# Retention's rotated queries and keys from one projection and a partition shuffle, and a plan that knows of wide GpSimd operations

## The chip, the cores and the metric

The kernel runs on one core of a Trainium2 chip. A core has a matrix engine (TensorE, PE in the profile), three engines for elementwise work (VectorE: DVE, ScalarE: ACT, GpSimd: POOL) and SyncE (SP), which here issues DMAs. The engines run side by side, each through its own instructions strictly in order, and wait for each other by semaphores. All work is in fp32. The metric is the device time of one execution in microseconds; the time before is 453.98 us, the median of three runs (452.66 to 454.3).

## The reference

Eight sequences of 256 tokens, 128 features each, go through eight residual steps, each behind a layer norm:

```
x = x + causal_attention(layernorm(x))     # 64-dimensional keys, one head
x = x + ffn_relu(layernorm(x))             # 512 hidden; ends in a layer norm of its own
x = x + linear_attention(layernorm(x))
x = x + ffn_relu(layernorm(x))
x = x + retention(layernorm(x))            # 16 heads
x = x + ffn_silu(layernorm(x))             # 384 hidden, int8-like weights
x = x + softmax_attention(layernorm(x))    # 16 heads of 8, LoRA weights
x = x + ffn_silu(layernorm(x))
```

The change is in retention. There queries and keys are rotated with the position:

```
def _rotate_every_two(x):
    x1 = x[..., ::2]
    x2 = x[..., 1::2]
    return jnp.stack((-x2, x1), axis=-1).reshape(x.shape)

def _theta_shift(x, sin, cos):
    return x * cos + _rotate_every_two(x) * sin

q = x @ q_w + q_b
k = (x @ k_w + k_b) * SCALING
qr = _theta_shift(q, sin, cos)
kr = _theta_shift(k, sin, cos)
```

So each rotated value needs its own value and that of its neighbour in the pair. The decay over positions is folded into the tables of sines and cosines, and the sign of the rotation into the table of sines.

## The kernel before

**Tiling.** The tokens are cut into four groups (GROUPS) of 512 tokens, two sequences each. A group's x is one tile of 128 partitions (tokens) by 4 x 128. Layers work on its transpose, 128 features by 512 tokens. Results of TensorE come in eight PSUM banks of 512 columns (`bank`), and are moved to SBUF by ScalarE or VectorE (L414 in `copied`). Other buffers come from stores: `work` (28), `small` (16), `wide` (6), `probs` (6), and the spread tiles `r_spread` and `l_spread`, which DMAs fill so that each head's queries and keys stand on partitions of their own (L761).

**The plan.** The order of all instructions is worked out when the program is built. Each layer of each group is a generator (`layers(g)`) that yields steps: an engine, or a choice of engines (`either`), and a cost in microseconds. The class `Plan` runs these generators against a clock of its own. At each turn it takes the step that can start first, and among those that can start on the same engine the one with the lowest rank; ranks are the hand-set numbers in RANKS, one for each group and layer, with FIRST, LAST and LATE for the rest. A step taken is written out at once, so that each engine's instruction order is the order in which the plan took the steps. For `either` the engine that could start first gets the work. Weights are prepared by threads with start times of their own (the `plan.start` lines at the end of `hybrid`). The plan's costs only set the order: on the chip every instruction waits for its data and nothing else.

**What lies near the change**, by line:

- `layernorm` (L503): statistics on VectorE (L511, L512), then four small operations on GpSimd (L518, L519, L522, L523; with `quick` the first two on VectorE), then per tile of 128 columns the normalisation, on ScalarE (L529) or VectorE (L534). `transposed` (L542) turns the result by TensorE (L550).
- Wide operations of GpSimd (128x512, or 128x272 in L903): `add_row_to` (L581), the biases and gamma of `ffn_relu` (L716, L752), the running sums of retention's states (L903), and some sums in `rotated` (L802).
- `ffn_relu`: up (L723, evicted by L726 or L728), down (L736, L742), a layer norm, gamma, and the residual sum L754 on VectorE.
- `retention` (L778): `rotated(i)` for queries (i = 0) and keys (i = 1). The weights hold four projections: queries, queries with the columns of each pair swapped, and the same for keys. Each is one matmul of 512 columns (L792), and VectorE adds the bias and multiplies by the table of cosines or sines while it moves the result out of PSUM (L794). GpSimd or VectorE adds the two parts (L802). Then come values (L822, L827), gates (L810, L812), the transposed keys (L875), states (L894, L881), scores by heads (L859, masked by L844), sums within and over chunks (L917, L939, L947) and a normalisation over the head (`finished`: L965 to L977, a square root by Newton steps, L767 to L776, transposition L986, gate L993, output L1002).
- Softmax attention: scores (L1135), maxima (L1156), exponentials (L1190), weighted sums (L1207), turned by L1220; projections L1249; FFN with silu: L1049, L1055, L1065.

Of the kernel before, what the change touches and what calls it, by code (L numbers as in the profile page):

```python
# [52 lines left out]
    "linear": [(32, 2, P), (P, D)],  # L53
    "retention_qk": [(P, 4, P), (P, 4, S), (P, 4)],
    "retention_vo": [(P, 512), (P, 256), (P, 2), (P, HEADS, VONE), (P, 2, D), (P, D)],
# [9 lines left out]
NEW_MODE = 0.09  # L65
LOAD = 0.1
ARRIVALS = (3.1, 5.1, 6.8, 8.3)
LEEWAY = 0.03


RANKS = [
    [-4.13, -2.77, -1.79, -1.45, 1.42, 1.01, -0.24, 3.83],
    [-1.82, 0.93, 5.08, 2.15, 1.79, 4.87, 0.66, 0.66],
    [-0.37, 1.61, -4.13, 2.32, 5.49, -4.05, 3.4, 4.38],
    [3.42, 6.69, 6.1, 9.09, 1.61, 0.82, 1.3, 1.92],
]
FIRST, LAST = -4.34, 9.59
LATE = 1.56


def of_act(n):
    return 0.05 + n / 1160
# [49 lines left out]
class Plan:  # L132
# [4 lines left out]
    def __init__(self):  # L137
        self.free = {e: 0.0 for e in (PE, ACT, DVE, POOL, SP)}
        self.steps = {e: [] for e in self.free}
        self.stores, self.untils, self.sleeping = [], [], []  # L140
        self.table = None
        self.mode = None
        self.current = None
        self.count = 0
        self.now = 0.0
# [20 lines left out]
    def put(self, store, *items, later=0.0):  # L166
        for item in items:
            self.count += 1
            store.items.append((self.current.after() + later, self.count, item))
# [30 lines left out]
    def joined(self, th):  # L200
        if th.join and all(j.done for j in th.join):
# [3 lines left out]
            self.go.append(th)  # L205

    def run(self):
        self.go = []
        while True:
# [12 lines left out]
            for e, queue in self.steps.items():  # L222
                if queue:
                    start = max(self.free[e], min(q[0] for q in queue))
                    if best is None or start < best[0]:
                        best = (start, e, None)
# [14 lines left out]
            if s is not None:  # L241
# [7 lines left out]
                continue  # L249
            able = [q for q in self.steps[e] if q[0] <= start]  # L250

# [16 lines left out]
            th.t, th.last = start + us, e  # L268
            self.free[e] = th.t
            self.resume(th, e)  # L270
        stuck = [s.waiting for s in self.stores if s.waiting] + self.untils
# [3 lines left out]
def step(engine, us, table=None, mode=None):  # L275
    return ("step", ((engine, us, table),), mode)


def either(*choices):
    return ("step", tuple((e, us, None) for e, us in choices), None)  # L280


def get(store, n=1):
    return ("get", store, n)


def join(threads):
    return ("join", list(threads))
# [11 lines left out]
def hybrid(ctx: ExitStack, tc: tile.TileContext, t: dict, out: bass.AP):  # L300
# [104 lines left out]
    def tokens(row, n):  # L405

        return row.unsqueeze(1).to_broadcast([P, n, row.shape[1]])
# [95 lines left out]
    def layernorm(src, y, quick=False):  # L503
# [21 lines left out]
        def half(tiles):  # L525
            for i in tiles:
                e = yield either((ACT, 0.39), (DVE, 0.25))
                if e == ACT:
                    nc.scalar.activation(  # L529
                        y[:, i, :], src[:, i, :], AF.Identity, bias=shift[:, i : i + 1],  # L530
                        scale=rstd[:, i : i + 1],
                    )
                else:
                    nc.vector.tensor_scalar(  # L534
                        y[:, i, :], src[:, i, :], mv[:, i, 0:1], rstd[:, i : i + 1],
                        ALU.subtract, ALU.mult,
                    )
# [41 lines left out]
    def add_row_to(g, row):  # L579
        yield step(POOL, 1.23)  # L580
        nc.gpsimd.tensor_tensor(x[g], x[g], tokens(row, NT), ALU.add)  # L581
# [126 lines left out]
    def ffn_relu(g):  # L708
# [5 lines left out]
        def biases():  # L714
            yield step(POOL, 1.23)
            nc.gpsimd.tensor_tensor(y4, y4, tokens(b2, NT), ALU.add)  # L716
            yield from add_row_to(g, beta)
# [32 lines left out]
        yield from layernorm(y4, y4)  # L750
        yield step(POOL, 1.23)
        nc.gpsimd.tensor_tensor(y4, y4, tokens(gamma, NT), ALU.mult)  # L752
        yield step(DVE, 0.6)
        nc.vector.tensor_tensor(flat(x[g]), flat(x[g]), y[:, :N], ALU.add)  # L754
# [23 lines left out]
    def retention(g):  # L778
# [4 lines left out]
        def rotated(i):  # L783

            part2 = yield get(work)
            a = qk[:, i, :], part2[:, :N]
            ps = yield get(bank, 2)

            def part(k):
                n = 2 * i + k  # L790
                yield step(PE, 0.86)
                nc.tensor.matmul(ps[k], w_ret_qk[:, n, :], yT[:, :N], start=True, stop=True)  # L792
                yield step(DVE, 0.66)
                nc.vector.scalar_tensor_tensor(  # L794
                    a[k].rearrange("p (b s) -> p b s", b=2), ps[k].rearrange("p (b s) -> p b s", b=2),
                    b_ret_qk[:, n : n + 1], tokens(rot_tab[:, n, :], 2), ALU.add, ALU.mult,
                )
                put(bank, ps[k])

            yield join([spawn(part(k)) for k in range(2)])  # L800
            e = yield either((POOL, 1.25), (DVE, 0.63))
            (nc.gpsimd if e == POOL else nc.vector).tensor_tensor(a[0], a[0], a[1], ALU.add)  # L802
            put(work, part2)
# [64 lines left out]
        def states(b, v, state):  # L868
# [32 lines left out]
            for n in range(1, 3):  # L901
                yield step(POOL, 0.73)
                nc.gpsimd.tensor_tensor(  # L903
                    state[n][:, :HV], state[n][:, :HV], state[n - 1][:, :HV], ALU.add
                )
# [51 lines left out]
        def finished(b, o, sq):  # L957
# [5 lines left out]
            den, var, root, tmp = (st[:, 32 * n : 32 * n + 32] for n in range(4))  # L963
            yield step(DVE, 1.03)
            nc.vector.tensor_scalar(  # L965
# [4 lines left out]
            put(work, sq)  # L970
            yield step(DVE, 2.35)
            newton_root(root, var, tmp)
            y = yield get(work)
            yield step(DVE, 0.6)
            nc.vector.scalar_tensor_tensor(
# [356 lines left out]
    for g in range(GROUPS):  # L1332
        plan.start(layers(g), g, ARRIVALS[g])
    plan.start(constants(), LAST, 31.1)
    plan.start(linear_weights(), LAST, 11.9)
    plan.start(retention_weights(), LAST, 47.5)
    plan.start(silu_weights(), LAST, 22.5)
    plan.start(softmax_weights(), LAST, 19)
    plan.start(pairs_of_scores(), FIRST, 0.0)
# [31 lines left out]
def _layout(i):  # L1371
    def swapped(a):

        return a.reshape(*a.shape[:-1], -1, 2)[..., ::-1].reshape(a.shape)

    q, qb, k, kb = (i[f"L1_attn_a_{n}"] for n in ("q_w", "q_b", "k_w", "k_b"))
    order = _by_head_rows()
    q, qs, k, ks = (a[..., order] for a in (q, swapped(q), k, swapped(k)))
    qb, qbs, kb, kbs = (a[order] for a in (qb, swapped(qb), kb, swapped(kb)))
    lora = {"q": order, "k": order, "v": np.arange(D)}  # L1380
# [5 lines left out]
    def chunks(a):  # L1386
# [15 lines left out]
        "retention_qk": (  # L1402
            np.stack([q, qs, k, ks], 1), _retention_tables(), np.stack([qb, qbs, kb, kbs], 1),
        ),
# [45 lines left out]
```

## Time and profile before

| | us |
|---|---|
| median of three runs | 453.98 |
| the profiled execution | 452.34 |
| its span | 450.5 |
| 16 projections for retention, L792, 32 instructions | 16.1 busy on TensorE |
| 16 rotations, L794 | 12.0 busy on VectorE |
| 8 sums, L802 | 6.8 busy on GpSimd (5), 3.0 on VectorE (3) |
| normalisations, L534 on VectorE (71) and L529 on ScalarE (89) | 30.6 and 38.9 busy |
| wide operations of GpSimd: L581 (16), L716 (8), L752 (8), L903 (16) | 20.4, 10.2, 10.2 and 12.3 busy |

A matmul in fp32 shows as two or more instructions, which overlap; the time of one is best read from when it and the next start. The groups of the profile give for each line the engine, the operation, the tiles (out<-in), the shapes, the count, the busy time, the mean of one, and the idle time of the engine just ahead of them with what ended it. The first and the last part of a page name the chain of work that ended last: followed back from the end, at each step, to whatever released it.

In the 40 slices of the span TensorE is at 9 tenths or more in all but the first and a few in the first 40%, GpSimd is busiest in the first third:

```
PE   7899899899999998999999999999999999999996
DVE  6997989787869985789998498869678656738443
ACT  3669735553433623513574773467963854783561
POOL 4154558765523562042222020320111100101101
```

### The profile page before, as it was taken

The numbers are of one execution on the slowest core, as the hardware profiler recorded it, in microseconds if no ns is written. First come the engines' busy times: TensorE is split into PE (matmuls) and PEld (weight loads), VectorE is DVE, ScalarE is ACT, GpSimd is POOL, SyncE is SP. The second block draws the span as 40 slices with busy tenths as digits, with TensorE's granted clock in tenths as the row PEclk, the third lists the DMA queues.
The fourth block names the chain that finished last, engine by engine and source line by source line (L and its number), as shares of the span: only waits on it lengthen the run. The fifth ranks groups of instructions, "written<-read, shape, count | busy, mean of one in ns | idle before, by whom it ended". The sixth has DMA issues, their size and how long they took to land.

```text
span 450.5 us, 13165 instructions
## 1 busy us (share of the span) xinstructions
PE 427.5 (95%) x5360; PEld 300.0 (67%) x5360; DVE 345.9 (77%) x992; ACT 245.0 (54%) x492; POOL 133.5 (30%) x239
## 2 busy tenths in 40 slices
PE   7899899899999998999999999999999999999996
PEld 6777677657677575685755665776765866566666
DVE  6997989787869985789998498869678656738443
ACT  3669735553433623513574773467963854783561
POOL 4154558765523562042222020320111100101101
PEclk9999899999999998999999999999999999999999
DMA  7300000003000300350000520000110001010001
GB/s 275 132 1 1 1 1 0 1 1 48 4 2 17 34 4 3 49 49 2 5 3 4 61 37 3 4 4 4 25 26 14 13 27 26 9 20 1 15 1 35
DMA packets 8043, 10.90 MB, mean 24 GB/s; under 512 B 1000, under 2 KB 6888, under 8 KB 7984
## 3 DMA queue, kind: packets, MB, share of 16 engines
q1 hardware_dynamic: 7904, 9.94, 10.7%
q8 instruction: 42, 0.69, 0.6%
q14 instruction: 17, 0.14, 0.1%
q10 hardware_dynamic: 80, 0.13, 0.1%
HBM read 4.56 MB, written 1.05 MB: 12 GB/s over the span
## 4 chain that ended last, share of the span: by engine, by line
PE 72%; DVE 18%; issue 4%; POOL 2%; ACT 2%; DMA 1%; SPq 0%; POOLq 0%; DVEq 0%; ACTq 0%
PE bank L1135 16%; PE bank L1207 7%; PE bank L1065 5%; PE bank L1049 5%; PE bank L859 4%; PE bank L736 4%; PE bank L1055 4%; PE bank L723 3%; DVE work L534 3%; DVE small L511 3%; PE bank L917 3%; DVE small L512 2%; PE bank L894 2%; PE bank L591 2%; PE bank L1220 2%
## 5 line engine op out<-in xcount | busy, mean ns | idle before, releaser
L1156 DVE TENSOR_REDUCE small<-bank 128x2 f32<-128x512 f32 x128 | 80.7, 684 | 15.2 <-PE bank L1135 14.4
L1135 PE MATMUL bank<-l_spread 32*128 32x256 f32 x1024 | 86.5, 401 | 0.0
L518 POOL TENSOR_SCALAR small<-small 128x4 f32<-128x4 f32 (+1 forms) x40 | 11.8, 295 | 242.7 <-DVE small L512 227.2
L1190 ACT ACTIVATE probs<-bank 128x512 f32<-128x512 f32 x128 | 67.7, 601 | 28.9 <-PE bank L1135 28.7
L414 ACT COPY work<-bank 128x512 f32<-128x512 f32 (+3 forms) x77 | 37.1, 492 | 68.1 <-PE bank L550 27.2
L1135 PEld LDWEIGHTS bank<-l_spread 32*128 32x128 f32 x1024 | 54.5, 184 | 25.7 <-issue 11.3
L522 POOL TENSOR_TENSOR small<-small,mhalf 128x4 f32<-128x4 f32 (+1 forms) x45 | 43.4, 965 | 6.8 <-DVE small L519 6.8
L529 ACT ACTIVATE work<-x,small 128x128 f32<-128x128 f32 x70 | 30.6, 487 | 26.6 <-POOL small L523 26.5
L511 DVE BATCH_NORM_STATS2 small<-x 128x6 f32<-128x128 f32 x128 | 34.7, 271 | 3.9 <-DMA x<-in_x 3.5
L414 DVE COPY work<-bank 128x256 f32<-128x256 f32 (+3 forms) x35 | 17.9, 521 | 22.8 <-PE bank L1207 12.3
L1207 PE MATMUL bank<-probs,l_values 128*32 128x256 f32 x512 | 33.2, 384 | 1.1 <-DVE work L1057 0.6
L736 PE MATMUL bank<-c_relu,work 128*128 128x128 f32 x256 | 32.4, 278 | 1.2 <-DVE work L728 1.2
L736 PEld LDWEIGHTS bank<-c_relu,work 128*128 128x128 f32 x256 | 30.3, 192 | 4.7 <-issue 2.4
L512 DVE BATCH_NORM_AGGREGATE small<-small 128x2 f32<-128x6 f32 x160 | 29.1, 182 | 5.5
L723 PE MATMUL bank<-work,c_relu 128*128 128x512 f32 x64 | 32.2, 618 | 0.1
L726 ACT ACTIVATE work<-bank,c_relu 128x512 f32<-128x512 f32 x26 | 17.9, 687 | 16.7 <-PE bank L723 15.7
L586 DVE TENSOR_TENSOR x<-bank,x 128x256 f32<-128x256 f32 (+1 forms) x36 | 16.1, 450 | 13.0 <-PE bank L1065 7.1
L1049 PE MATMUL bank<-work,c_ints 128*128 128x256 f32 (+1 forms) x72 | 25.3, 463 | 0.7 <-ACT work L414 0.7
L1065 PE MATMUL bank<-c_ints,work 128*128 128x128 f32 x192 | 24.6, 279 | 0.5 <-ACT work L414 0.5
L1051 ACT ACTIVATE work<-bank 128x256 f32<-128x256 f32 (+1 forms) x36 | 15.7, 454 | 16.7 <-PE bank L1049 16.4
L1065 PEld LDWEIGHTS bank<-c_ints,work 128*128 128x128 f32 x192 | 22.9, 192 | 2.7 <-issue 1.1
L1055 PE MATMUL bank<-work,c_ints 128*128 128x256 f32 (+1 forms) x72 | 24.6, 458 | 0.0
(151 smaller groups left out, 797.6 us busy)
## 6 DMA issues: line engine op xcount, KB each, us to landing
r_spread<-wide SPq DMA_DIRECT2D x32, 64.0 KB
l_spread<-wide SPq DMA_DIRECT2D x32, 64.0 KB
out<-x SPq DMA_DIRECT2D x8, 128.0 KB
c_retention_qk<-in_retention_qk SPq DMA_DIRECT2D x1, 770.0 KB
x<-in_x SPq DMA_DIRECT2D x3, 256.0 KB
c_retention_vo<-in_retention_vo SPq DMA_DIRECT2D x1, 713.0 KB
c_relu<-in_relu SPq DMA_DIRECT2D x1, 706.0 KB
c_ints<-in_ints SPq DMA_DIRECT2D x1, 576.0 KB
```

What stands on the lines that cost most here:

```text
L414: (nc.scalar.copy if e == ACT else nc.vector.tensor_copy)(dst, src)
L511: nc.vector.bn_stats(stats[:, i, :], src[:, i, :])
L522: nc.gpsimd.tensor_tensor(rstd, rstd, minus_half[:, :nt], ALU.pow)
L723: nc.tensor.matmul(ps, w1[:, c * P : (c + 1) * P], yT[:, :N], start=True, stop=True)
L736: nc.tensor.matmul(ps[:, n * D : (n + 1) * D], h[c][:, i * P : (i + 1) * P], w2[:, c, :], start=(c == 0), stop=(c == 3),)
L1049: nc.tensor.matmul(ps[:, :n], w_gate[:, cols], yT[:, :n], start=True, stop=True)
L1055: nc.tensor.matmul(ps[:, :n], w_up[:, cols], yT[:, :n], start=True, stop=True)
L1065: nc.tensor.matmul(ps[:, (i - first) * D : (i - first + 1) * D], h[c][:, i * P : (i + 1) * P], w_down[:, c, :], start=(c == 0), stop=(c == 2),
L1135: nc.tensor.matmul(to[k][:, n * S : (n + 1) * S], seq.spread[rows, j, of_keys, n * P : (n + 1) * P], seq.spread[rows, j, 1 - of_keys, :], ...
L1156: nc.vector.tensor_reduce(nmax[:, h2 % 4 // 2, 2 * (h2 % 2) + k, :], ps[k].rearrange("p (m s) -> p m s", m=2), AX.X, ALU.max, negate=True,)
L1190: nc.scalar.activation(p[:, k, :], ps[k], AF.Exp)
L1207: nc.tensor.matmul(o[32 * i : 32 * (i + 1), (j % 2) * S : (j % 2 + 1) * S], seq.v[:, c, VONE * h : VONE * h + 32], seq.p[h2][0][:, k, c * ...
```

## The change

The change has three parts.

1. In `rotated` queries and keys are projected once each, with their biases added on the way out of PSUM by ScalarE or VectorE. The swapped values are then made in SBUF by a shuffle of partitions on VectorE: features are laid out so that the two of a pair stand four partitions apart within 32. Two multiplications by the tables and the sum follow, each on GpSimd or VectorE. One PSUM bank is held instead of two. The packed weights, the biases and the layout lose their swapped halves, so that this load has 641 KB instead of 770.

2. The plan has a mark `PORT`. Wide operations of GpSimd carry it, and so do the steps of VectorE that read and write SBUF alone: L534, L754, L965 to L977 with the Newton steps, the shuffle, and the multiplications and sums of `rotated`. While a marked step runs on GpSimd in the plan's time, a marked step on VectorE can't start there; `either` then may give it to the other engine, or another step is taken first.

3. The numbers that steer the plan are others: all RANKS, FIRST, LAST, LATE, LEEWAY (how much later than its last reader a score bank counts as free) and the start times of the threads for weights and constants.

```diff
@@ class Plan
+        self.port = 0.0
...
+    def ready(self, engine, q):
+        return max(q[0], self.port) if engine == DVE and q[1].mode == PORT else q[0]
...
-                    start = max(self.free[e], min(q[0] for q in queue))
+                    start = max(self.free[e], min(self.ready(e, q) for q in queue))
...
-            able = [q for q in self.steps[e] if q[0] <= start]
+            able = [q for q in self.steps[e] if self.ready(e, q) <= start]
...
             self.free[e] = th.t
+            if e == POOL and th.mode == PORT:
+                self.port = th.t
...
@@ layernorm
-                e = yield either((ACT, 0.39), (DVE, 0.25))
+                e = yield either((ACT, 0.39), (DVE, 0.25), mode=PORT)
...
@@ add_row_to; the same mark at L715, L751, L753, L902, L964, L971, L974
-        yield step(POOL, 1.23)
+        yield step(POOL, 1.23, mode=PORT)
...
@@ retention, rotated(i)
-            part2 = yield get(work)
-            a = qk[:, i, :], part2[:, :N]
-            ps = yield get(bank, 2)
-
-            def part(k):
-                n = 2 * i + k
-                yield step(PE, 0.86)
-                nc.tensor.matmul(ps[k], w_ret_qk[:, n, :], yT[:, :N], start=True, stop=True)
-                yield step(DVE, 0.66)
-                nc.vector.scalar_tensor_tensor(
-                    a[k].rearrange("p (b s) -> p b s", b=2), ps[k].rearrange("p (b s) -> p b s", b=2),
-                    b_ret_qk[:, n : n + 1], tokens(rot_tab[:, n, :], 2), ALU.add, ALU.mult,
+            part1, part2 = qk[:, i, :], (yield get(work))
+            ps = yield get(bank)
+            yield step(PE, 0.86)
+            nc.tensor.matmul(ps, w_ret_qk[:, i, :], yT[:, :N], start=True, stop=True)
+            e = yield either((ACT, of_act(N)), (DVE, of_dve(N)))
+            if e == ACT:
+                nc.scalar.activation(part1, ps, AF.Identity, bias=b_ret_qk[:, i : i + 1])
+            else:
+                nc.vector.tensor_scalar(part1, ps, b_ret_qk[:, i : i + 1], None, ALU.add)
+            put(bank, ps)
+
+            yield step(DVE, 0.65, mode=PORT)
+            nc.vector.stream_shuffle(part2[:, :N], part1, [p ^ KDIM // 2 for p in range(32)])
+
+            def times(k, a):
+                e = yield either((POOL, 1.25), (DVE, 0.63), mode=PORT)
+                a = a.rearrange("p (b s) -> p b s", b=2)
+                (nc.gpsimd if e == POOL else nc.vector).tensor_tensor(
+                    a, a, tokens(rot_tab[:, 2 * i + k, :], 2), ALU.mult
                 )
-                put(bank, ps[k])
-
-            yield join([spawn(part(k)) for k in range(2)])
-            e = yield either((POOL, 1.25), (DVE, 0.63))
-            (nc.gpsimd if e == POOL else nc.vector).tensor_tensor(a[0], a[0], a[1], ALU.add)
+
+            yield join([spawn(times(k, a)) for k, a in enumerate((part1, part2[:, :N]))])
+            e = yield either((POOL, 1.25), (DVE, 0.63), mode=PORT)
+            (nc.gpsimd if e == POOL else nc.vector).tensor_tensor(
+                part1, part1, part2[:, :N], ALU.add
+            )
             put(work, part2)
...
@@ the numbers of the plan
-LEEWAY = 0.03
+LEEWAY = 0.04
...
-    [-4.13, -2.77, -1.79, -1.45, 1.42, 1.01, -0.24, 3.83],
+    [-0.77, -1.96, -6.09, -0.44, -1.22, -2.97, -2.46, 4.75],
...
-FIRST, LAST = -4.34, 9.59
-LATE = 1.56
+FIRST, LAST = -3.5, 11.25
+LATE = 0.91
...
-    plan.start(retention_weights(), LAST, 47.5)
-    plan.start(silu_weights(), LAST, 22.5)
-    plan.start(softmax_weights(), LAST, 19)
+    plan.start(retention_weights(), LAST, 15.6)
+    plan.start(silu_weights(), LAST, 16.5)
+    plan.start(softmax_weights(), LAST, 43.2)
```

In the built program the instructions of retention's rotation fall like this; apart from them, 21 normalisations stand on ScalarE that stood on VectorE, and the order on every engine is another from the first layers on.

| | before | after |
|---|---|---|
| projections on TensorE | 16 | 8 |
| evictions with the bias | 16 on VectorE, times the table | 7 on ScalarE, 1 on VectorE |
| shuffles on VectorE | 0 | 8 |
| multiplications by a table | in the eviction | 9 on GpSimd, 7 on VectorE |
| sums | 5 on GpSimd, 3 on VectorE | 4 on GpSimd, 4 on VectorE |
| normalisations | 71 on VectorE, 89 on ScalarE | 50 and 110 |

Lines are named by their numbers in the kernel before.

## The prediction

> **What bounds the kernel now.** I read the engines' shares first, then the chain of work that ended last, then the stretches.
>
> ```profile
> PE 427.5 (95%) x5360; PEld 300.0 (67%) x5360; DVE 345.9 (77%) x992; ACT 245.0 (54%) x492; POOL 133.5 (30%) x239
> ...
> PE 72%; DVE 18%; issue 4%; POOL 2%; ACT 2%; DMA 1%; SPq 0%; POOLq 0%; DVEq 0%; ACTq 0%
> ```
>
> TensorE is at work for 427.5 of 450.5 us and holds 72% of the chain; VectorE has 18%. The time is TensorE's work plus some 23 us in which it stands. The stretches of 15 us say where (after the bounds: busy PE, PEld, DVE, ACT, POOL, then granted clock, DMA share, GB/s):
>
> ```profile
> 45.00:60.00 15.00, 13.14 (x70) 9.13 (x69) 13.55 (x44) 10.51 (x23) 9.28 (x16) 0.89 0.00 1
> 75.00:90.00 15.00, 13.18 (x90) 10.50 (x90) 12.49 (x45) 7.96 (x18) 12.36 (x23) 1.00 0.01 1
> 90.00:105.00 15.00, 14.24 (x63) 8.73 (x61) 12.83 (x33) 8.23 (x13) 10.59 (x14) 1.00 0.09 16
> 165.00:180.00 15.00, 12.85 (x345) 8.67 (x346) 9.38 (x17) 4.37 (x11) 6.57 (x6) 0.89 0.02 4
> 195.00:210.00 15.00, 15.00 (x226) 9.73 (x228) 14.05 (x32) 3.51 (x7) 5.30 (x9) 1.00 0.26 26
> ```
>
> From 180 us on TensorE is nearly full; its idle time lies ahead of that, where VectorE and GpSimd are busiest, and at the two ends. Twice, behind a stall, the granted clock is down: 0.89 over 15 us is a loss of 1.7 us each time.
>
> Next the lines that the change touches, by line and form (count | busy us, mean ns | idle before), then the spread of single durations (min/median/max):
>
> ```profile
> L792 PE MATMUL bank<-work,c_retention_qk 128*128 128x512 f32 x32 | 16.1, 633 | 0.0
> L529 ACT ACTIVATE work<-x,small 128x128 f32<-128x128 f32 x70 | 30.6, 487 | 26.6 <-POOL small L523 26.5
> L802 POOL TENSOR_TENSOR wide<-wide,work 128x512 f32<-128x512 f32 x5 | 6.8, 1353 | 22.0 <-DVE work L794 22.0
> ```
>
> ```profile
> L534 DVE TENSOR_SCALAR work<-x,small x58: 315/342/1305, 6.6 to 441.2; 128x128 f32<-128x128 f32 x58
> ...
> L802 POOL TENSOR_TENSOR wide<-wide,work x5: 1265/1277/1652, 98.1 to 245.1; 128x512 f32<-128x512 f32 x5
> L802 DVE TENSOR_TENSOR wide<-wide,work x3: 691/693/1597, 99.8 to 176.2; 128x512 f32<-128x512 f32 x3
> ...
> L794 DVE SCALAR_TENSOR_TENSOR wide<-bank,c_retention_qk x8: 739/746/752, 96.4 to 243.6; 128x512 f32<-128x512 f32 x8
> ```
>
> VectorE's L534 takes 0.34 us, but up to 1.3; L802 takes 0.69, once 1.6. L794, whose first input is in PSUM, never strays. The timeline shows what the long ones meet (start, length):
>
> ```profile
> 58.88 1.27 POOL L581 TENSOR_TENSOR x<-x,c_relu 128x512 f32<-128x512 f32 x1
> 58.95 1.74 DVE L754 TENSOR_TENSOR x<-x,work 128x512 f32<-128x512 f32 x1 [0.28 <-POOL work L752]
> ```
>
> The sum of VectorE begins 0.07 us behind GpSimd's, and ends 0.54 us after it. So it stood for about 1.05 us and then took its 0.69. Going through all instructions of L534, L754, L802 and L975 by what GpSimd ran beside them, I count about 15 that were held like this, 12 us in all.
>
> **The change, part by part.**
>
> *TensorE.* Eight of the 16 projections of 512 columns go. Four of them stand from 95.37 us to the next line at 98.81: 0.86 us each. So 8 × 0.86 = 6.9 us of the bounding engine go. The stages they come from (90 to 260 us) have TensorE full for most of their length, so I take all of it: −6.9.
>
> *VectorE.* Out go 16 L794 at 0.75 (12.0 us) and three L802 at 0.69 (2.1 us). In come, by the order of the built kernel, one eviction (0.69), eight shuffles, seven multiplications and four sums at 0.69. No row shows a shuffle. The nearest is L968, a reduction that reads 128x512 from SBUF, at 0.68; below lies L534's 0.34 for a quarter of the columns, above a held L802 at 1.6. I take 0.69 as for L802: 20 × 0.69 = 13.8 us, against 14.1 before. VectorE gets neither better nor worse by this part. The order further moves 21 of the 71 L534 to ScalarE (−7.2 us).
>
> On the shuffle, "VectorE: DVE Perf Modes" of the Trainium skill (the perf-mode tier table) gives about 2400 ns for 2048 columns, one mode only; a quarter is an estimate of 0.6 us, and eight would be 4.8 us instead of 5.5. No row here shows it.
>
> *ScalarE.* Seven evictions at 0.59 (4.1), 21 normalisations at 0.487 (10.2), two more table loads at 1.28 (2.6), less four L726 at 0.69: +14 us on an engine with 205 us idle. Cost 0: what hides it is that idle time; without it, the 2.6 us of table loads would stand in front of the exponentials.
>
> *GpSimd.* 13 wide operations of retention instead of five: 8 × 1.27 = +10.2 us on an engine that is 30% busy. They come in rows: three for the first retention in TensorE's order, four for the second, five for the third, one for the fourth. Behind each row stand small operations of a layer norm (L518 to L523), for which ScalarE waits (26.5 us in the line above), and behind it a transposition on TensorE. In the second to fourth retention TensorE has, between the projection and the transposed keys (L875), whole score blocks and FFN pieces of other groups, 15 us and more. In the first it has 12 L736 (1.3 us), four transpositions (0.4), two L723, two L810 and four L822 (1.7 each): 6.9 us. VectorE's queue there is eviction, two shuffles, multiplication, two L742 at 0.42, multiplication, four pairs of statistics at 0.45, then the last sum: 0.69 × 6 + 0.84 + 1.8 = 6.8 us. That is just covered; handoffs may open 0 to 1.3 us, and shuffles at the upper bound 2 × 0.9 more. I take +0.4.
>
> *The port in the plan.* A VectorE step marked so is not placed while a marked wide GpSimd step runs; no wait is added to the program, only the order is another, with new ranks and start times for all work. What it can win is that part of the 12 us for which TensorE stood: 1.8 us of waiting on L534 itself and 0.7 at 61 us behind the held L754, 2.5 in all; with one drop of the clock (the stall ends at 52.3 us, the clock falls at 53.4) 4.2. The lower bound is 0, if the next wait follows at once. I take −1.5.
>
> Against this speaks "SBUF — State Buffer" of the skill (two separate sides): the shared pair is one exclusive lock, but only a two-port mode or two SBUF inputs take it. The rows agree that others are not held: L968 stays within 672 to 684 ns and L774 within 191 to 194. By that rule the plan holds shuffles and Newton steps back for nothing, up to 1.27 us each; if all eight shuffles paid this on TensorE's path, the sum would be 10 us higher.
>
> *Loads.* The first constants shrink from 770 to 641 KB; TensorE waits for x alone at the start (3.3 us), so 0.
>
> *Sum.* The profiled execution took 452.34 us, 450.5 of span and 1.84 around it. 452.34 − 6.9 − 1.5 + 0.4 = 444.3. The median of the runs shown, 453.98, lies 1.64 above that execution: 446.0.
>
> **The rivals.**
>
> *More is won* (0.18). The held operations vanish from the chain and neither drop of the clock returns: −6.9 − 4.2 − 1.7 = 439.5, with 1.64 some 441. For it: the idle time lies where GpSimd is busiest. Against: most stalls are under 1 us and have other causes too (L414, L728).
>
> *TensorE's saving turns into waiting* (0.13). From the last projection to the rotated tensor it was 0.75 + 1.27 = 2.0 us; now 0.59 + 0.69 + 1.27 + 1.27 = 3.8. If each of four retentions laid its 1.8 us bare, +7.2 − 6.9 gives 452.6, or 454.3 as a median. For it: VectorE's 18% of the chain. Against: other groups' work between.
>
> *Slower: GpSimd's rows* (0.11). In-order rows of wide operations ahead of the layer norms' small ones; eight more at 1.27 are 10.2 us, and two drops of the clock behind such stalls 3.4: 13.6 − 6.9 = +6.7, 459.0, as a median 461. It decides from 9.2 us of these 13.6 on. For it: GpSimd runs at 12.36 of 15 us in 75 to 90 already. Against: the longer rows come later, where it has 5 to 8 of 15.
>
> **How the numbers follow.** My forecast, a gain with 443 to 450 as its own range, has 0.58. Half a per cent, 2.3 us, is about what a measurement can tell here. Faster: 0.58 + 0.18 = 0.76; the same: 0.13; slower: 0.11. For 8 in 10 the range goes down to 440 and up to 453.5, which leaves out the slower case and the upper half of the unchanged one.
>
> **What would show it.** TensorE busy near 420.6 us, or the removed 6.9 us back as idle time. Shuffles near 0.69 us. Few L534 over 0.5 us, and 12 us held shrinking to 3 or less. The wait of L875 in the first retention under 1.3 us. What makes it wrong: idle time of TensorE over 30 us, in stalls behind L523 or the multiplications on GpSimd, or a third stretch at half clock.

## The result, and the profile after

Twelve runs of each kernel on one chip gave a median of 454.35 us after (452.32 to 461.53) and 453.45 before (451.37 to 454.55). The ratio is 1.0025, with a 95% interval of 1.0002 to 1.0049: 0 to 0.5% slower, within the half per cent that the prediction took for no change. (Every ratio here leaves out runs more than 1.5% above the fastest of their kernel, as the one of 461.53 us.) The forecast was 446.0 and its range ended at 453.5. What came has the number of the rival "TensorE's saving turns into waiting", 454.3, but not its place; that the number fits is luck.

The profiled execution of after took 453.16 us (span 451.0; before 452.34 and 450.5). From here on lines have the numbers of the changed kernel: L536 and L541 are the normalisations on ScalarE and VectorE (L529, L534 before), L557 turns them, L588 is `add_row_to`, L723 and L759 the sums and products of `ffn_relu` on GpSimd, L761 its residual sum, L781 to L783 the Newton steps. In `rotated` L795 projects, L798 and L800 evict, L804 shuffles, L809 multiplies and L815 adds. L874 are the score matmuls (L859), L932 the sums within a chunk (L917), and in `finished` L984 ends the denominators, L990 (L975) makes the product and L1001 (L986) turns it.

The engines' shares and the chain of waits of after:

```profile
PE 426.1 (94%) x5344; PEld 301.2 (67%) x5344; DVE 336.4 (75%) x980; ACT 258.6 (57%) x522; POOL 142.8 (32%) x247
...
PE 79%; DVE 11%; issue 3%; POOL 3%; ACT 2%; DMA 0%; POOLq 0%; DVEq 0%; ACTq 0%
```

VectorE fell by 9.5 us, and its share of the chain from 18% to 11%. But TensorE's busy time fell by 1.4 us only, from 427.5. The eight projections did go. The lines of the rotation, by line and form (count | busy us, mean ns | idle before):

```profile
L795 PE MATMUL bank<-work,c_retention_qk 128*128 128x512 f32 x16 | 8.5, 623 | 0.2 <-ACT work L421 0.2
...
L804 DVE STREAM_SHUFFLE work<-wide 128x512 f32<-128x512 f32 x8 | 5.8, 732 | 0.0
```

The projections stand at 8.5 us busy where they stood at 16.1, so 7.6 went there and 6.2 came back elsewhere as busy time. Up to half of that is the clock: L730 took 1,057 to 1,061 ns at half clock (a granted clock of 0.5) and 592 ns as a rule, and time at half clock grew from two stretches of 3.41 us to four, besides one in the last 1.2 us of before. Where the rest came from these rows don't show. The stretches of after show where half clock and idle time lie (bounds: busy PE, PEld, DVE, ACT, POOL, granted clock, DMA share, GB/s):

```profile
45.00:60.00 15.00, 13.83 (x76) 9.78 (x75) 11.53 (x41) 11.36 (x28) 10.06 (x16) 0.89 0.00 1
75.00:90.00 15.00, 14.48 (x92) 10.97 (x91) 10.13 (x35) 9.07 (x20) 11.87 (x18) 1.00 0.00 1
...
120.00:135.00 15.00, 10.44 (x402) 8.53 (x402) 7.89 (x22) 5.31 (x14) 4.51 (x4) 1.00 0.10 20
...
150.00:165.00 15.00, 14.06 (x319) 9.47 (x311) 10.53 (x30) 4.88 (x10) 5.77 (x11) 0.77 0.01 3
...
180.00:195.00 15.00, 13.46 (x92) 10.70 (x93) 12.64 (x38) 3.61 (x9) 9.15 (x12) 0.89 0.34 44
```

The first two are a little fuller than before (13.14 and 13.18 of 15 there). The loss is later: 4.6 us of idle time at 120 to 135, and half clock after 150 and after 180. Over three long stretches, for before and then for after:

```profile
0.00:105.00 105.00, 94.49 (x542) 71.17 (x543) 90.53 (x316) 63.62 (x134) 60.69 (x110) 0.98 0.14 47
105.00:195.00 90.00, 84.86 (x1494) 61.34 (x1493) 71.80 (x223) 35.00 (x76) 34.00 (x54) 0.98 0.15 20
```

```profile
0.00:105.00 105.00, 97.15 (x560) 73.62 (x561) 84.27 (x315) 68.08 (x149) 62.33 (x112) 0.98 0.12 43
105.00:195.00 90.00, 81.38 (x1483) 60.91 (x1483) 72.63 (x220) 37.88 (x82) 45.45 (x65) 0.94 0.16 24
```

Count as lost what TensorE stood, and half of the time at half clock. Up to 105 us both have one half-clock stretch of 3.41 us, and the loss fell from 10.5 + 1.7 to 7.9 + 1.7: 2.7 us gained. From 105 to 195 us it rose from 5.1 + 1.7 to 8.6 + 5.1 (clock 0.94 is 10.24 us at half): 6.9 us, as much as the projections were to save. The same stretch of time doesn't hold the same work in both kernels, so this says where time is lost and not yet why.

Two waits of TensorE lead that stretch. One is for its own instructions ("issue"). The timeline of after (start, length, idle time ahead and its releaser):

```profile
122.02 1.35 PE L932 MATMUL bank<-work,r_values 64*32 64x64 f32 x113
125.09 1.52 PE L932 MATMUL bank<-work,r_values 64*32 64x64 f32 x128 [1.72 <-issue]
128.82 0.34 PE L932 MATMUL bank<-work,r_values 64*32 64x64 f32 x15 [2.21 <-issue]
```

The profile shows nothing that these matmuls waited for. The other is for VectorE, and this timeline of after has its cause:

```profile
170.47 1.09 POOL L588 TENSOR_TENSOR x<-x,c_retention_vo 128x512 f32<-128x512 f32 x1
170.82 0.79 DVE L984 TENSOR_TENSOR small<-small 128x32 f32<-128x32 f32 x1
172.25 1.30 POOL L588 TENSOR_TENSOR x<-x,c_softmax 128x512 f32<-128x512 f32 x1 [0.69 <-DVE small L774]
172.46 1.14 DVE L781 TENSOR_TENSOR small<-small 128x32 f32<-128x32 f32 x1
173.52 1.26 POOL L723 TENSOR_TENSOR work<-work,c_relu 128x512 f32<-128x512 f32 x1
173.64 1.19 DVE L782 SCALAR_TENSOR_TENSOR small<-small 128x32 f32<-128x32 f32 x1
174.74 1.26 POOL L588 TENSOR_TENSOR x<-x,c_relu 128x512 f32<-128x512 f32 x1
174.86 1.19 DVE L783 SCALAR_TENSOR_TENSOR small<-small 128x32 f32<-128x32 f32 x1
176.09 0.19 DVE L781 TENSOR_TENSOR small<-small 128x32 f32<-128x32 f32 x1
...
181.54 0.67 PE L1001 MATMUL bank<-ident,work 128*128 128x128 f32 x3 [2.44 <-DVE work L990]
```

A Newton step takes 0.19 us. Here four steps in a row each wait for a wide operation of GpSimd and end just after it: 0.60 + 0.95 + 1.00 + 1.00 = 3.55 us late. A second such chain follows on VectorE, then L990 for both, and TensorE stands 2.44 us for it; the next 3.41 us it runs at half clock.

The marks were there to prevent this, and the diff shows why they didn't: `ready` holds only VectorE back, and `port` is set only by GpSimd. A GpSimd step may start while a marked step of VectorE runs, and the plan books the 11 instructions of a square root as one step of 2.35 us, long enough for a whole operation of GpSimd to fall into it. The words on the plan above, that on the chip every instruction waits for its data and nothing else, don't hold either: the four steps had their data, and so, as far as the profile shows, had L932.

### The profile page after: what moved, and what is told of

It reads as the page before. It is cut to its first block, busy times and chain, and to the rows that moved or that the text cites. A ratio compares the mean times of both kernels' runs of the same rounds, so it can differ in the third digit from the quotient of the medians.

```text
span 451.0 us, 13156 instructions
## 1 busy us (share of the span) xinstructions
PE 426.1 (94%) x5344; PEld 301.2 (67%) x5344; DVE 336.4 (75%) x980; ACT 258.6 (57%) x522; POOL 142.8 (32%) x247
## 4 chain that ended last, share of the span: by engine, by line
PE 79%; DVE 11%; issue 3%; POOL 3%; ACT 2%; DMA 0%; POOLq 0%; DVEq 0%; ACTq 0%
PE bank L1150 17%; PE bank L1222 7%; PE bank L1064 5%; PE bank L1080 5%; PE bank L730 4%; PE bank L1070 4%; PE bank L874 4%; PE bank L743 3%; PE bank L932 3%; PE bank L557 3%; PE bank L598 2%; PE bank L909 2%; PE bank L1235 2%; PE bank L1017 2%; PE bank L962 2%
## 5 line engine op out<-in xcount | busy, mean ns | idle before, releaser
L1150 PE MATMUL bank<-l_spread 32*128 32x256 f32 x1024 | 84.1, 400 | 0.0
L525 POOL TENSOR_SCALAR small<-small 128x4 f32<-128x4 f32 (+1 forms) x40 | 10.4, 260 | 210.4 <-DVE small L519 209.1
L421 ACT COPY work<-bank 128x512 f32<-128x512 f32 (+3 forms) x87 | 41.3, 485 | 45.0 <-PE bank L557 16.2
L536 ACT ACTIVATE work<-x,small 128x128 f32<-128x128 f32 x86 | 37.2, 487 | 29.4 <-POOL small L530 29.0
L529 POOL TENSOR_TENSOR small<-small,mhalf 128x4 f32<-128x4 f32 (+1 forms) x45 | 43.4, 964 | 7.1 <-DVE small L526 7.1
L730 PE MATMUL bank<-work,c_relu 128*128 128x512 f32 x64 | 33.1, 639 | 2.0 <-ACT work L421 1.4
L1064 PE MATMUL bank<-work,c_ints 128*128 128x256 f32 (+1 forms) x72 | 26.4, 486 | 0.5 <-DVE work L421 0.5
L1080 PE MATMUL bank<-c_ints,work 128*128 128x128 f32 x192 | 26.1, 281 | 0.5 <-DVE work L1072 0.4
L557 PE MATMUL bank<-ident,work 128*128 128x128 f32 x128 | 22.8, 297 | 2.5 <-ACT work L536 2.4
L1070 PE MATMUL bank<-work,c_ints 128*128 128x256 f32 (+1 forms) x72 | 24.7, 461 | 0.1
L1222 PEld LDWEIGHTS bank<-probs,l_values 128*32 128x32 f32 x512 | 13.8, 109 | 15.2 <-issue 4.5
L557 PEld LDWEIGHTS bank<-ident,work 128*128 128x128 f32 x128 | 15.9, 148 | 11.8 <-ACT work L536 6.1
```

The source lines that it names most:

```text
L421: (nc.scalar.copy if e == ACT else nc.vector.tensor_copy)(dst, src)
L529: nc.gpsimd.tensor_tensor(rstd, rstd, minus_half[:, :nt], ALU.pow)
L557: nc.tensor.transpose(ps[:, i * P : (i + 1) * P], y[:, i, :], ident)
L730: nc.tensor.matmul(ps, w1[:, c * P : (c + 1) * P], yT[:, :N], start=True, stop=True)
L1064: nc.tensor.matmul(ps[:, :n], w_gate[:, cols], yT[:, :n], start=True, stop=True)
L1070: nc.tensor.matmul(ps[:, :n], w_up[:, cols], yT[:, :n], start=True, stop=True)
```

## The experiments

A ratio is to runs of the kernel before on the same chip at the same time. The 454.35 us of after come from runs of their own, beside which before had 453.45; differences to after are taken between the two ratios, and are good to some 1.5 us.

**The projections alone.** `v_before_cut` takes half of TensorE's projection work from the kernel before, in before's own order:

```diff
-nc.tensor.matmul(ps[k], w_ret_qk[:, n, :], yT[:, :N], ...)
+cols = N if k == 0 else 8
+nc.tensor.matmul(ps[k][:, :cols], w_ret_qk[:, n, :], yT[:, :cols], ...)
```

> The kernel before, in its own order; the eight swapped projections have 8 columns instead of 512 (504 columns of each swapped half are left out, so what is rotated is not the reference's). If TensorE's work is on the path where it was removed, about 6.5 us go: 447 us, ratio near 0.985. If the projections lie under other waits, less than 2 us go: 452 us or more, ratio above 0.995.

It took 452.32 us against 453.18, ratio 0.9977 (0.9955 to 0.9999): about 1 us for some 6.6 us of TensorE's work, at the same mean clock (0.994). `v_after_twice` is the opposite, each projection of after issued twice (`for _ in range(2):` in front of the matmul):

> The changed kernel, in its own order; each of the eight projections is issued twice, so that TensorE has the work of 16 again. If TensorE's work is on the path, about +7 us against the changed kernel: 460 to 462 us, ratio near 1.017. If the removed work had only been turned into waiting, the doubled matmuls fill waits: under +2 us, 454 to 456, ratio below 1.006.

455.33 us, ratio 1.004 (1.0012 to 1.0068): 0.7 us above after, which is within the noise. But the clock differs: it is 0.988 on average over these twelve runs, and 0.98 over those of after. Runs at the same clock are 3 us apart (0.981: 457.1 to 457.8 us against 454.1; 0.989: 455.0 to 456.4 against 452.3 and 452.8). So in before's order the eight projections are worth 1 us; in after's it is 3 us at one clock, of which most came back with a higher clock. In neither is it 6.9. Where the time goes in `v_before_cut` its waits of TensorE show, here behind those of before (us in total, times, longest):

```profile
PE bank L917 <- issue: 5.0, 6, 2.1
...
PE bank L986 <- DVE work L975: 0.6, 2, 0.4
```

```profile
PE bank L918 <- issue: 6.3, 7, 2.0
...
PE bank L987 <- DVE work L976: 2.2, 2, 1.7
```

L917 and L918 are L932 of after, L986 and L987 its L1001: TensorE reached the same two waits earlier, and stood there. They take 2.9 us of the 4.4 by which its idle time grew.

**The parts of the change alone.** `f_rot` has the new rotation with before's numbers and without marks, `f_num` the new numbers alone, each a part of the diff shown above.

> The one projection, the shuffle and the multiplications alone, with the old numbers of the plan and no marks for the port; the plan makes its own order from it. If the loss is in the new numbers and marks, this is the gain as forecast: 445 to 448 us, ratio 0.982 to 0.989. If the rotation itself costs what it saves (longer path, GpSimd's rows), 451 to 456, ratio 0.995 to 1.005. If the order is luck, anything between 445 and 460.

> The kernel before with the new ranks, leeway and start times alone. These numbers belong to another set of steps, so I expect a worse order: 455 to 465 us, ratio 1.005 to 1.025. If the new numbers are better whatever the steps, under 452, ratio below 0.997.

The ratios are 1.0887 (490.94 and 497.06 us) and 1.0262 (465.75 us). It seems that numbers found for one set of steps make a bad order for another. Neither run isolates its part: what they tell is that a changed order moves the time by more than any edit here, so the runs below keep the order of their kernel.

**Newton steps.** One iteration of three (`for _ in range(1)` in `newton_root`; the square roots are coarser), in before, in before with the cut projections, and in after:

> The kernel before in its own order, with one of the three Newton iterations for retention's square root (two are left out: 6 small VectorE instructions of 0.19 us in each of eight sequences, 9 us of VectorE's work). The control for the next: if that chain ends in waits of TensorE, 2 us or more go (under 451.5); if TensorE covers it in the order of before, under 1 us.

> As before, with both cuts: the swapped projections at 8 columns, and one Newton iteration of three. Theory: what TensorE lost was covered by VectorE's chain and by the supply of instructions, so that the two cuts are worth more together than alone: 448 us or less, ratio under 0.989. Rival: the cuts just add (about -1 of the projections and what the control shows): 451 to 452.

> The changed kernel in its own order with one Newton iteration of three. Theory: its longest wait on data, 2.4 us at 179 us for the end of two such chains, goes, and with it the half clock behind it: 3 to 4 us less than the changed kernel, 450 to 451.5, ratio 0.992 to 0.996. Rival (VectorE's chain covers nothing, only the supply of instructions counts): within 1 us of the changed kernel, ratio 1.000 to 1.005.

Before: 451.9 against 452.67, ratio 0.9986 (0.9971 to 1.0001). Both cuts: 449.64, 0.994 (0.9916 to 0.9964), 3.0 us where the two alone gave 0.8 and 0.9, though the interval, 1.6 to 3.8 us, holds their plain sum too. After: 447.37, 0.9891 (0.9859 to 0.9923), 6 us less than after, with a mean clock of 0.986 for 0.98. The same cut is worth nothing that can be measured in the one kernel and 6 us in the other, so VectorE's chain is on the path in after and hardly in before. With two iterations in after:

> The changed kernel in its own order, with two of three Newton iterations (one is left out). If the end of two Newton chains at 179 us is what TensorE waits for, a third less of the chain (2 x 3 x 0.19 = 1.2 us of 2.4) gives about half of what two iterations less gave: 3 us less than the changed kernel, 450 to 452, ratio 0.994 to 0.997. If the gain of n_after came by the clock alone, all or nothing: 447 to 448.5 or 453 to 454.

450.79 us, 0.9947 (0.9925 to 0.9969), 3.5 us less than after. Read so, the chain's own length is the cause. But the first iteration of the chain shown above is still held in `n_after` (L782 up to 1,191 ns): fewer steps take the wait away just as unheld ones would, so these runs don't tell the two apart.

**The held steps alone.** `x_row` cuts the four operations of GpSimd above to 8 columns and leaves everything else as in after:

```diff
+rows.append(g)
+n = 2 if len(rows) in (10, 11, 12) else D
-nc.gpsimd.tensor_tensor(x[g], x[g], tokens(row, NT), ALU.add)
+nc.gpsimd.tensor_tensor(x[g][:, :, :n], x[g][:, :, :n], tokens(row, NT)[:, :, :n], ALU.add)
```

(and the same for the eighth b2 sum, L723).

> After, with four wide operations of GpSimd cut from 512 to 8 columns, so that they are there but take almost no time: the sum that met L984 at 170.5 us (L588) and the row of three that met the Newton steps from 172.25 us on (L588, L723, L588). Their sums are not what the reference has. GpSimd stands idle for 6.7 us behind them, so that their own 4.9 us are worth nothing. In after, L984 and three Newton steps took 0.79 to 1.19 us there instead of 0.19: 3.6 us late on VectorE, and TensorE waited 2.44 us for this chain. Theory (the held port, in a place that the marks leave open, makes the wait): the four steps take 0.19 us, the wait at L1001 goes, and with it the half clock that follows: 2.4 to 4.1 us less, 450.2 to 452.0 at a median of 454.35 for after. Rival (the chain's own nine steps per square root make it, and the held port is hidden): the wait stays above 1.5 us and the median at 453.8 to 454.9. Second rival (TensorE's instructions are late next): the wait goes, waits on issue grow by as much, and the median stays.

449.5 us, ratio 0.9921 (0.9894 to 0.9948), below the theory's range. GpSimd then stands idle for 6.6 us, so the operations' own time is not what was saved. The long stretch of `x_row`:

```profile
105.00:195.00 90.00, 83.11 (x1513) 61.80 (x1512) 73.54 (x229) 41.91 (x90) 44.22 (x68) 1.00 0.18 25
```

The timeline of `x_row` at the transposition that waited:

```profile
176.48 1.29 DVE L996 SCALAR_TENSOR_TENSOR work<-work,small 128x512 f32<-128x512 f32 x2
...
178.24 1.04 PE L1007 MATMUL bank<-ident,work 128*128 128x128 f32 x8
```

L996 is L990 of after. It starts 4.2 us earlier than there, 3.5 of them by the four steps, which take 0.19 us each again. Nothing stands idle in front of the transposition, and from 105 to 195 us no half clock is left. TensorE loses 6.9 us in this stretch where after loses 13.7 and before 6.9: the whole saving is back, in this execution. But the profiled run, 446.95 us at a clock of 0.992, is one of the three fastest of twelve, and over all of them the clock is 0.984 on average (after 0.98): part of the gain in this profile was luck with the clock. The ratios put the four operations at 4.7 us.

**The same with all the work done.** `x_late` computes the reference as after does, and moves three of the four operations to where no Newton step runs. `chains` holds the b2 sum (L723), which the new small operation makes wait for y; `kept` holds the L588 with c_relu and, to be taken second, the one with c_softmax:

```diff
@@ finished, behind the product y (L990)
+ended.append(b)
+if len(ended) == 4:
+    nc.gpsimd.tensor_tensor(tmp[:, :4], y[:, :4], y[:, :4], ALU.mult)
+    for add in chains:
+        add()
+    chains.extend([None] * 4)
...
@@ layernorm, behind L530; sums has one entry for each L815 on GpSimd
+if len(sums) == 4:
+    late.append(src)
+    if len(late) == 1:
+        kept.pop()()
+    if len(late) == 3:
+        kept.pop()()
```

> After, with all of its work, and three of GpSimd's wide operations moved to where no Newton step runs: the b2 sum (L723) waits for the end of the second Newton chain, by a small operation that reads its product (L990), the sum with c_relu (L588) comes behind the next layer norm's small operations, the one with c_softmax behind the one after the next but one; the sum that met L984 stays. Theory (the held Newton steps are worth some 4 to 5 us, as they were with these operations cut to 8 columns, 449.5): no Newton step over 0.25 us at 172 to 176 us, no wait of over 0.5 us at L1001 there, 449.5 to 451.5, faster than both kernels. Rival (what GpSimd no longer does early it does in front of the small operations of layer norms, and TensorE waits there instead): waits on L536 grow by 2 us or more and the median is 453 or higher.

451.03 us, ratio 0.9952 (0.9934 to 0.997): faster than both kernels, as the theory expected, by 3.3 us against after; at the same clock by 2 to 3 us (0.985: 450.7 to 451.1 us against 452.8 to 453.2; 0.981: 450.8 to 452.5 against 454.1). Its timeline (L1013 is L990, L1030 is L1001, L1019 the new small operation, L739 is L723):

```profile
179.42 1.28 DVE L1013 SCALAR_TENSOR_TENSOR work<-work,small 128x512 f32<-128x512 f32 x2
...
180.59 1.04 PE L1030 MATMUL bank<-ident,work 128*128 128x128 f32 x8
...
180.78 0.20 POOL L1019 TENSOR_TENSOR small<-work 128x4 f32<-128x4 f32 x1 [7.56 <-DVE work L1013]
180.93 1.28 POOL L739 TENSOR_TENSOR work<-work,c_relu 128x512 f32<-128x512 f32 x1
```

The row of three is gone from the Newton steps, and TensorE no longer stands in front of the transposition. The waits that the rival named grew by 1.1 us on ScalarE (29.9 to 31.0) and not at all on TensorE (2.4). By mean less median, the groups of VectorE that are late by more than 0.3 us come to some 6 us, as against 8.2 in after (13.1 before). Not all of the loss is gone in this execution: TensorE stands for 6.9 us from 105 to 195 us, as in before, but half clock, now from 129.6 and 153.5 us on, still takes 5.1:

```profile
105.00:195.00 90.00, 83.11 (x1494) 61.95 (x1492) 70.79 (x221) 38.23 (x84) 44.70 (x66) 0.94 0.17 24
```

**TensorE's instructions.** In `d_half_within` every second L932 is left out (`range(0, 4, 2)`; 1,024 of TensorE's instructions and half of the sums within a chunk):

> The changed kernel in its own order with every second of the small matmuls of L917 (there L932) left out: 256 of 512, 1,024 of TensorE's 10,800 instructions, 6.6 us of its work. Theory: these stretches wait for instructions, which come in packets of 16 KB at no less than 3.44 us; then the waits named issue (6.8 us) fall to under 2.5, and the time by more than the cut work: 444 to 449, ratio under 0.990. Rival: only the work counts, as with the projections: 452 to 454, and the issue waits stay.

443.31 us, 0.9806 (0.9774 to 0.9838): 10 us less than after. The line's busy time fell by 4.2 us (14.1 to 9.9), not by the 6.6 expected, and the mean clock rose to 0.99. The waits of TensorE in after, and then here:

```profile
PE bank L932 <- issue: 5.2, 3, 2.2
...
PE bank L874 <- issue: 1.6, 2, 0.9
```

```profile
PE bank L1001 <- DVE work L990: 2.7, 1, 2.7
...
PE bank L932 <- issue: 1.5, 1, 1.5
...
PE bank L874 <- issue: 0.7, 1, 0.7
```

The waits for instructions shrink from 5.2 + 1.6 to 2.2 us, so 4.6 us come with the work; the wait for VectorE (2.4 in after) stays. Both sources are real, and separate.

**The clock.** `e_fill` adds 14 matmuls of 128 columns in front of the transposition that waits, so that TensorE's idle time is filled:

> The changed kernel in its own order, with 14 extra matmuls of 128 columns (1.5 us) in front of the transpositions for which TensorE waits 2.4 us at 179 us; nothing reads them. If the half clock behind it comes from the idle time, it goes there and the kernel gets faster by 0.5 to 1.7 us with more work: ratio 0.999 to 1.002, mean clock up by 0.003 or more. If the clock falls for another reason: no change or up to 0.5 us slower, ratio 1.002 to 1.004, the same mean clock.

452.12 us, 0.9987 (0.9968 to 1.0006): 1.7 us less than after, though TensorE has 3.1 us more work. The mean clock of the twelve runs is 0.985 against 0.98. In the profile the half clock behind 181.8 us is gone, but the one at 151.0 stands at 126.4, and another of 6.83 us came at 280.0. So a part of what the held steps cost was paid in the clock, as far as 1.7 us with an error of 1.4 can tell.

**Other plans.** Three plans that also follow the supply of TensorE's instructions, with numbers chosen anew by each plan's own clock:

> After's rotation with another plan: the plan follows the supply of TensorE's instructions (256 in 3.45 us), the marks hold on both sides (a marked step of GpSimd waits for a marked one of VectorE too), the shuffle is not marked, and all numbers are chosen anew. Theory (the projections' 6.9 us are lost to the order, in waits on instructions, on held Newton steps and in half clock): waits on issue at L932 and L874 under 3 us together, few VectorE steps held, 443 to 450. Rival (numbers found on the plan's own clock don't carry over to the chip): 455 or more, as with the rotation alone and with the numbers alone.

> The same plan as in the kernel above with the rotation of before (16 projections, no shuffle), its numbers chosen anew for as long. Theory (with an order made for each, one rotation is worth little more than the other, as 6.6 us of projections were worth 1 us alone): within 4 us of the kernel above. Rival (the projections are worth their 6.9 us once the order fits): 5 us or more above it.

> As the first of these plans, but the marks hold on one side as in after, and the Newton steps are not marked at all. Theory (held Newton steps cost time on the chip): slower than with marks on both sides, by 2 us or more, with VectorE's steps late by over 10 us in all. Rival (holding GpSimd back for the marks costs more than the held steps): faster than it.

470.24 us (ratio 1.0389), 457.99 (1.0112) and 453.04 (1.001). In the first and the third it was the rival that came: the plan with marks on both sides gave the worse order, and the plan without marks on the Newton steps was as fast as before, with some 10 us late on VectorE. In the second neither came: the old rotation did better by 12 us. A better account of the chip in the plan did not by itself give a better order. Which rotation is the better one under equally good plans stays open.

## Why the prediction was wrong, step by step

**TensorE: −6.9 "taken in full".** This step failed. The work went (7.6 us of busy time on the line), but its removal is worth 1 us in before's order (`v_before_cut`), and in after's 0.7 us as measured and 3 at the same clock (`v_after_twice`). The reason given, that TensorE is full for most of these stages, is no proof that its work sets their end: it was full, and still reached waits whose ends something else sets, instructions and VectorE's chains.

**The clock: no term.** The sum counted on less half clock at best, and on none more; two further drops stood in a rival alone. After's runs have a mean clock of 0.98, those of before beside the experiments 0.994 to 0.995. Among the runs of after itself 0.008 of clock go with 1.8 us (452.32 at 0.989, 454.11 at 0.981), so that this is worth some 3 us. Two runs of before with so low a clock, 0.989 and 0.988, took 454.9 and 454.5 us, where after took 452.3 and 452.8 at 0.989: at one clock the change gains about 2 us. This is read from runs that differ by themselves; only `e_fill` moved the clock by intent.

**The port in the plan: −1.5.** Its place was right and its mechanism half right. Up to 105 us the loss fell by 2.7 us, in the range of 0 to 4.2, and normalisations of over 0.5 us fell from twelve of 71 to three of 50; that the marks did this, and not the new numbers, no run shows. But the step took the marks to shrink the 12 us held to 3 or less, and they shrank to 8.2 (from 13.1 by the same count). The description that it worked from, a marked step "is not placed while a marked wide GpSimd step runs", was true, and it never asked about the other direction. The 3.55 us held in a row at 170 to 176 us cost 3.3 us (`x_late`, which frees three of the four) to 4.7 us (`x_row`).

**The objection drawn from "SBUF — State Buffer" of the Trainium skill.** The page (two separate sides) says that a VectorE instruction with two inputs in SBUF contends with a GpSimd instruction that reads SBUF. The prediction concluded that Newton steps are held back for nothing, because L774 had stayed within 191 to 194 ns. They have two such inputs, and had met no wide operation of GpSimd before. In after L781 took 1,142 ns. The page was right and was misread; for the shuffle, with one input, the conclusion holds (718 to 752 ns in all eight), though only one of them, 724 ns at 184.0 us, ran beside a wide operation.

**VectorE's sum.** 13.8 us in for 14.1 out; it was 16.5 in (0.8, 5.8, 6.5 and 3.4) for 15.0 out: the shuffle at 0.73 instead of 0.69, the eviction at 0.75, and L809 and L815 late by 2.3 us in all. The engine came out 9.5 us lighter all the same, by the normalisations: 16.4 us after 30.6, where 7.2 less was forecast.

**ScalarE and GpSimd.** +13.6 us and +9.3 us as forecast (14 and 10.2). The first retention's cover held: L890, the transposition of the keys (L875), waited 0.43 us against a bound of 1.3. The row that hurt was not retention's: it was bias sums beside Newton steps.

**The list of what would show it.** TensorE busy near 420.6 was not seen, in part because half clock stretched the rest. Nor was the "removed 6.9 us back as idle time": over the whole span idle time grew by 1.9 us (23.0 to 24.9), and time lost to half clock by some 3. Few long normalisations, the short wait of L890 and the third stretch at half clock were seen. The rival that came nearest laid the waiting at the rotation, 1.8 us for each retention; it lay at `finished` and at the sums within a chunk.

**A tally** from the runs: −1.0 for the projections, −2.7 for the first 105 us (one execution of each kernel), +3.3 to +4.7 for the held steps with their clock, together −0.4 to +1.0, where +0.9 was measured. It fits, but each term is uncertain by 1 us or more, and no run took the marks alone at a fixed order: the second term is read and not tested, and how much the new numbers by themselves add or take stays open.

## What to carry to other kernels

Before the whole of a removed piece of work is counted, make it shorter in place or issue it twice: one run told that 6.6 us of a 95% busy engine were worth 1. Then compare runs at the same granted clock: the projections that were issued twice seemed to cost 0.7 us, and cost 3. Look at the single longest instance of a line and not at its mean: 0.23 us for a Newton step looked harmless, and three instances of 1.2 us in a row set the end of a stage. A rule that keeps two engines apart has to hold in both directions, and a step that stands for many small instructions leaves as many places in which they can meet.

## What the runs showed of the hardware

**TensorE's instructions come in packets.** The page of after counts them:

```profile
q8 instruction: 42, 0.69, 0.7%
```

42 packets of 16,384 bytes for some 10,800 instructions, about 256 in each. Two of them never start closer than 3.44 us in the traces of before and after (3.31 in all the runs). Blocks of L874 and L932 are 128 instructions, and where nothing waits one starts 0.6 to 1.0 us after another, so several in a row use 256 in less than the time between two packets. Every "issue" wait of TensorE of over 0.4 us in these two traces ends at instruction 256·k + 449, 2.3 to 2.8 us after the start of a packet. The instruction ahead of the wait starts at 121.3, 124.5, 170.6, 218.0, 225.6 and 297.8 us in before, at 120.8, 123.2, 126.4, 150.3 and 230.0 in after. So I read these waits as the supply of instructions, which small matmuls side by side outrun; `d_half_within` agrees, with 2.2 us of them instead of 6.8.

**The clock falls without a gap of 3 us, and not behind each stall.** In after half clock begins at 52.1, 151.0 and 181.8 us, at steps of 3.413 us from each other (29 and 9 of them), and lasts 3.41 or 6.83 us. In the 3.41 us ahead of 181.8 TensorE was busy for 0.97 us; in those ahead of 151.0 for 2.87, and the wait of 0.94 us in which it then stood had lasted for 0.54. In `e_fill` it was busy for 3.17 us ahead of 280.0. Two windows of the same steps, from 123.7 and 127.2 us in after, with 1.52 and 1.75 us of work, had no half clock behind them. "TensorE: Matmul & The Clock Gate" in the Trainium skill (why this matters for your kernels) advises to leave no gaps over about 3 us, behind which the clock goes back to half. The half speed agrees with these rows, but no single wait ahead of these falls was longer than 2.44 us. The twelve runs of after follow the clock: 452.32 us at 0.989, 454.11 at 0.981, 458.59 at 0.966.
